# Two graph layers on one core: adjacency combined among the third graph's queries, outputs added a step later, scales reordered, tail in halves

## The chip, the cores and the metric

The kernel runs on one core of a Trainium2 chip. The metric is the time on the device in microseconds (us), from the first to the last instruction of the core. A core has five engines with an instruction queue each: TensorE (PE: matmuls, transposes), VectorE (DVE), ScalarE (ACT), GpSimd (POOL) and SyncE (SP, which here only issues transfers). Each runs its own instructions in the order in which the program gives them, and waits on semaphores for the others. Transfers run on 16 DMA engines.

## What is computed

Sixteen graphs `x` of 1024 nodes with 256 channels go through two layers; everything is float32. Cut to what matters:

```python
# layer 0, for each graph
h = relu(layernorm(x))
c = mean of h over channels
Wg = adj * A_s(c[m] - c[n])              # a weight for each pair of nodes
q = relu((h^T @ Wg) * para)              # queries, four heads of 64
k, v = h @ kv_w
x = x + softmax(q k^T * scale) v         # attention among 1024 nodes

# layer 1
h = relu(layernorm(x))
agg = A_hat @ h                          # A_hat: adj + I, scaled by degrees, the same for all graphs
y = agg @ W1.T + b1
y = relu(batchnorm(y))                   # statistics over all nodes of all graphs
out = batchnorm(y @ W2.T + b2)           # again over all graphs
x = x + out
```

The batch norms need all sixteen graphs before they can scale anything. So the kernel has a first stage (`layers`: layer 0, and layer 1 up to the matmul with W1, graph by graph), a second stage (`second`: the products with W2), and a tail that scales, transposes and adds.

## The kernel before

**First stage.** TensorE alternates between the attention of graph b and pieces of background work for other graphs. A graph has four units (two pairs of heads, two halves of the queries), a unit four steps. A step makes scores, finishes what is due, multiplies the step before's exponentials with the values, and then takes background pieces until their share of TensorE's time is used up:

```python
for s in range(len(steps) + 2):
    ...
        made = scores(*unit.at, g)            # TensorE, then exp on ScalarE
        due = total * (s % per_graph + 1) / per_graph
    finished, ended = ended, None
    if finished is not None:
        finished.finish()                     # transposes of the unit's output, added to x
    if top:
        done += advance(bg)
    ...
        for pr in made:
            unit.add(pr)                      # VectorE sums the exponentials
    if before is not None:
        (last, g_last), prs = before
        last.values(g_last, prs)              # TensorE; the last one copies o to os
        if g_last == NG - 1:
            last.divide()                     # sums, four reciprocals, os * inv
            ended = last
    while done < due and not top:
        cost = advance(bg)                    # a piece of background work
        ...
    if finished is not None:
        finished.watch()                      # two reductions over the reciprocals
```

Background work is made of generators; `weave(main, (start, side), ...)` takes one piece of each side after every piece of the main one, and what is left of the sides at the end. While graph 1's attention runs, the third graph's queries, keys and values are made, and the normalized adjacency is made once for all graphs:

```python
def background(b):
    ...
    gather = aggregate(b - 1)
    if b + 1 < B:
        whole = graph() if b == 1 else nothing
        yield from weave(queries(b + 1), (0, weighers[b + 1]), (0, islice(whole, 16)))
        if b > 1:
            yield next(gather)
        yield from weave(keys_values(b + 1), (0, normed(b - 1)), (0, whole))
        if b == 1:
            yield next(gather)
```

`queries` has 16 pieces, `keys_values` 8. The first piece of `gather` issues the first three loads of adjacency. `graph()` makes the adjacency in eight units. Products with it use a scheme of seven multiplications for a product of 2 by 2 blocks (in place of eight), so differences of its blocks are stored with it, in `aht_d` in HBM:

```python
def graph():
    for t in range(HT):                       # 4
        for part in range(2):
            a = p4.tile([P, 2, NH, HB], F32, tag="adj", ...)      # one of four buffers
            for n in range(2):
                nc.sync.dma_start(out=a[:, n], in_=adj_t...)
            yield 0.0
            for n in range(2):
                ...                           # + identity, * degrees: VectorE
            sub(two[:, 0], b12, a[:, 0, 0])   # sub: GpSimd
            sub(two[:, 1], b22, two[:, 0])
            yield 0.0
            sub(b12, b22, b12)
            sub(one, b21, two[:, 1])
            nc.gpsimd.dma_start(out=dst[:, :4], in_=a...)
            nc.gpsimd.dma_start(out=dst[:, 4:6], in_=two)
            nc.gpsimd.dma_start(out=dst[:, 6], in_=one)
            yield 0.0
```

The four buffers `adj` also hold the blocks of `adj` that `weigh` multiplies with the pair weights (tile `w`, line 382, VectorE), which `queries` uses, and later the pieces `aht` that `aggregate` loads. The banks for `queries` (`pg`) are two; VectorE frees one by writing `q` from it.

**Second stage.** It begins with combinations of W2's blocks on GpSimd, then the scales of the first batch norm, whose square root is on GpSimd as well (`rsqrt`, lines 82 and 83):

```python
nc.gpsimd.tensor_add(s1, a21, a22)
nc.gpsimd.tensor_sub(s2, s1, a11)
nc.gpsimd.tensor_sub(s3, a11, a21)
nc.gpsimd.tensor_sub(s4, a12, s2)
aff = []
for half in range(2):
    r = slice(half * JH, (half + 1) * JH)
    aff.append(affine(mv1[:, r], g1[:, r], be1[:, r], f"1{half}"))
```

Then ScalarE scales and clips `yin`, and TensorE makes seven products for each graph (line 997).

**Tail.** The second batch norm's scales, then graph by graph: scale the whole of both channel halves (1024 nodes each), transpose, add to the graph `xo` of the first layer (loaded from `x1_d`), and store. Up to eight graphs `xo` are held; the ninth is loaded once a store has freed a buffer:

```python
for k in range(CC):
    nc.vector.bn_aggr(mv2[:, k, :], ...)
s2, sh2 = affine(mv2, g2, be2, "2")
for b in range(B):
    while len(xos) < min(b + 8, B):
        load_x1()
    xo = xos[b]
    for k in range(CC):
        nc.scalar.activation(y2[b][k], y2[b][k], AF.Identity, bias=..., scale=...)
    for g in range(NT // 2):
        ...                                   # four transposes
        nc.vector.tensor_add(dst, pt, dst)
    nc.gpsimd.dma_start(out=out[b]..., in_=xo)
```

Of the kernel before, what the change touches and what calls it, by code (L numbers as in the profile page):

```python
# [10 lines left out]
F32 = mybir.dt.float32  # L11
# [6 lines left out]
P = 128  # L18
# [5 lines left out]
def gnn_two_layers_kernel(  # L24
# [60 lines left out]
    def layers(shifted):  # L85
# [135 lines left out]
        def graph():  # L221


            HT, HB = NT // 2, FB // 2
            for t in range(HT):
                for part in range(2):
                    cols = slice(part * HB, (part + 1) * HB)
                    a = p4.tile([P, 2, NH, HB], F32, tag="adj", name=f"au_{t}_{part}")
                    for n in range(2):
                        r = slice((t + n * HT) * P, (t + n * HT + 1) * P)  # L230
                        nc.sync.dma_start(
                            out=a[:, n], in_=adj_t[r].rearrange("p (m c) -> p m c", m=NH)[:, :, cols]
                        )
                    yield 0.0
                    for n in range(2):
                        if part == t * P // HB:
                            blk = a[:, n, n, t * P % HB : t * P % HB + P]
                            nc.vector.tensor_add(blk, blk, ident)
                        nc.vector.tensor_mul(
                            a[:, n], a[:, n], dbc.rearrange("p (m c) -> p m c", m=NH)[:, :, cols]  # L240
                        )
                    two = py.tile([P, 2, HB], F32, tag="y", name=f"two_{t}_{part}")
                    one = py.tile([P, HB], F32, tag="y", name=f"one_{t}_{part}")
                    b12, b21, b22 = a[:, 0, 1], a[:, 1, 0], a[:, 1, 1]
                    sub = nc.gpsimd.tensor_sub
                    sub(two[:, 0], b12, a[:, 0, 0])
                    sub(two[:, 1], b22, two[:, 0])
                    yield 0.0
                    sub(b12, b22, b12)
                    sub(one, b21, two[:, 1])  # L250
                    dst = aht_d[:, t // TH, :, t % TH, cols].rearrange("i p c -> p i c")
                    nc.gpsimd.dma_start(out=dst[:, :4], in_=a.rearrange("p n m c -> p (n m) c"))
# [3 lines that stand above are left out]
# [357 lines left out]
        def background(b):  # L613

            nothing = iter(())
            if b == 0:
                yield from prepare(1, nothing)
                yield from weave(queries(1), (0, weighers[1]), (1, degrees()))
                cbs = columns_of(dinv, "deg")
                if B > 2:  # L620
                    load_x(2)
                    yield from weave(keys_values(1), (1, Norm(2, True).all()))
                else:
                    yield from keys_values(1)
                yield TOP
                broadcast_row(dbc, cbs, "deg")
                yield 1.0
                if B > 2:
                    yield from prepare(2, nothing)
                return  # L630
            before = hidden(b - 1)
            gather = aggregate(b - 1)
            if b + 1 < B:
                whole = graph() if b == 1 else nothing
                yield from weave(queries(b + 1), (0, weighers[b + 1]), (0, islice(whole, 16)))
                if b > 1:
                    yield next(gather)
                yield from weave(keys_values(b + 1), (0, normed(b - 1)), (0, whole))
                if b == 1:
                    yield next(gather)  # L640
            else:
                yield from weave(endings.pop(), (2, normed(b - 1)))
                yield next(gather)
            if b + 2 < B:
                yield from weave(gather, (7, Norm(b + 2, True).all()))
                yield from prepare(b + 2, before)
            elif b + 2 == B:

                yield from gather
                endings.append(before)  # L650
            else:
                yield from gather
                yield from weave(before, (0, normed_last()))
# [156 lines left out]
        def attention():  # L810
# [1 line left out]
            units = [Unit(b, k, f) for b in range(B) for k in range(CC) for f in range(NH)]  # L812
            steps = [(u, g) for u in units for g in range(NG)]
            per_graph = CC * NH * NG
            before = ended = None
            bg, done, total, top = iter(()), 0.0, 0.0, False
            for s in range(len(steps) + 2):
                if s < len(steps):
# [11 lines left out]
                    due = total * (s % per_graph + 1) / per_graph  # L830
                else:
                    due += 5.1
                finished, ended = ended, None
                if finished is not None:
                    finished.finish()
                if top:
                    done += advance(bg)
# [4 lines left out]
                if before is not None:  # L842
                    (last, g_last), prs = before
                    last.values(g_last, prs)
                    if g_last == NG - 1:
                        last.divide()
                        ended = last
                while done < due and not top:
                    cost = advance(bg)
                    if cost is None:  # L850
                        break
                    if cost == TOP:
                        top = True
                        break
                    done += cost
                    if ended is not None and cost > 1.0:
                        ended.behind_piece()
# [41 lines left out]
    def second(kind):  # L899
# [5 lines left out]
        io = st.enter_context(tc.tile_pool(name=f"io_{kind}", bufs=4))  # L905
        ps = st.enter_context(tc.tile_pool(name=f"ps_{kind}", bufs=4, space=PSUM))

        def affine(mv, gamma, beta, name):

            n = mv.shape[1]  # L910
            sm = wp.tile([P, 4, n], F32, name=f"sm_{name}")
            s, sh, rstd, tmp = (sm[:, i, :] for i in range(4))
            rsqrt(rstd, mv[:, :, 1], EPS, tmp)
            nc.vector.tensor_mul(s, rstd, gamma)
            nc.vector.tensor_mul(sh, mv[:, :, 0], s)
            nc.vector.tensor_sub(sh, beta, sh)
            return s, sh

        xos = []

        def load_x1():


            b = len(xos)
            pool, tag = ((xp, "xo"), (io, "yin"), (wp, "both"))[(b % 8 > 2) + (b % 8 > 6)]
            xo = pool.tile([P, NT, C], F32, tag=tag, name=f"xo_{kind}_{b}")
            nc.sync.dma_start(out=xo, in_=x1_d[b])
            xos.append(xo)

        with st:  # L930
            JH = HC // 2


            a11, a12, a21, a22 = (
# [5 lines left out]
            nc.gpsimd.tensor_sub(s2, s1, a11)  # L940
            nc.gpsimd.tensor_sub(s3, a11, a21)
            nc.gpsimd.tensor_sub(s4, a12, s2)
            aff = []
            for half in range(2):
                r = slice(half * JH, (half + 1) * JH)
                aff.append(affine(mv1[:, r], g1[:, r], be1[:, r], f"1{half}"))
            b2_step = wp.tile([P, 1], F32, name="b2_step")
            nc.vector.tensor_sub(b2_step, b2[:, 1:2], b2[:, 0:1])
            ys, t1s, t2s, y2 = {}, {}, {}, []
# [52 lines left out]
            def graph(b, ahead):  # L1002
# [31 lines left out]
                add(c12, product(f"m3_{b}", s4, b22), c12)  # L1034
                stats(1, 1, c22)
                next(ahead, None)
                add(c21, product(f"m4_{b}", a22, t2s[b]), c21)
                stats(0, 1, c12)
                stats(1, 0, c21)
                next(ahead, None)  # L1040

            def ahead_of(b):
# [15 lines left out]
                        load_y(2 * b + 2 + i)  # L1058
                yield

            for i in range(4):
                load_y(i)

# [14 lines left out]
                if kind == "f" and b == B // 2 + 2:  # L1078
                    flag(ps.tile([P, FB], F32, tag="pz", name=f"good_{kind}")[:, 0:1])

            mv2 = wp.tile([P, CC, 2], F32, name="mv2")
            for k in range(CC):
                nc.vector.bn_aggr(mv2[:, k, :], stats2[:, k].rearrange("p a s -> p (a s)"))
            s2, sh2 = affine(mv2, g2, be2, "2")
            for b in range(B):
                while len(xos) < min(b + 8, B):
                    load_x1()
                xo = xos[b]
                for k in range(CC):
                    nc.scalar.activation(  # L1090
                        y2[b][k],
                        y2[b][k],
                        AF.Identity,
                        bias=sh2[:, k : k + 1],
                        scale=s2[:, k : k + 1],
                    )
                for g in range(NT // 2):
                    pt = ps.tile([P, 2, C], F32, tag="pz", name=f"pt_{kind}_{b}_{g}")
                    for j in range(2):
                        t = 2 * g + j  # L1100
                        for k in range(CC):
                            nc.tensor.transpose(
                                pt[:, j, k * P : (k + 1) * P],
                                y2[b][k][:, t * P : (t + 1) * P],
                                ident,
                            )
                    dst = xo[:, 2 * g : 2 * g + 2, :]
                    nc.vector.tensor_add(dst, pt, dst)  # L1108
                nc.gpsimd.dma_start(out=out[b].rearrange("(t p) c -> p t c", p=P), in_=xo)

    fp = ctx.enter_context(tc.tile_pool(name="fp", bufs=1))
    bad = fp.tile([1, 1], mybir.dt.int32, name="bad")
# [61 lines left out]
```

## Time and profile before

| | |
|---|---|
| time, median of three runs | 2741.65 us (2741.38 to 2742.55) |
| span of the profiled execution | 2741.2 us |
| TensorE's mean granted clock | 0.986 |
| HBM read, written | 278.41 MB, 74.45 MB |
| start of the attention, of the second stage's matmuls, end of those | about 65, 2464.2, 2660 us |

A line of the waits reads: the waiting engine, tile and source line, what ended the wait, us in total, how many waits, the longest. A line of the timeline reads: start, duration, engine, source line, operation, output and inputs, shapes, count, and in brackets the idle time of the engine ahead of it and what ended it. A row of the stage table gives the busy time of each engine in a stretch, then TensorE's granted clock, the share of the DMA engines and what they moved in GB/s. A 128x512 line is 128 partitions of 512 elements.

### The profile page before, as it was taken

How to read it: one execution, taken by the hardware profiler on the slowest of the kernel's cores; microseconds unless marked ns; L12 is line 12 of the kernel's file. 1: busy time of each engine (PE TensorE's matmuls, PEld its weight loads, DVE VectorE, ACT ScalarE, POOL GpSimd, SP SyncE). 2: the span in 40 equal slices, each digit the busy share in tenths (PEclk: the TensorE clock that was granted, in tenths of full speed). 3: DMA queues.
4: the chain of work that ended last, by engine and by line, in shares of the span. 5: the costliest groups of instructions: out<-in, count | busy, mean ns of one | idle time of the engine just before them, and what ended most of it. 6: DMA issues, size and time to landing. Idle time of an engine off the chain costs nothing.

```text
span 2741.2 us, 31973 instructions
## 1 busy us (share of the span) xinstructions
PE 2622.6 (96%) x12106; PEld 972.1 (35%) x12106; DVE 1741.1 (64%) x2621; ACT 1293.1 (47%) x1843; POOL 349.2 (13%) x410
## 2 busy tenths in 40 slices
PE   7997999999999999999999999999999999989985
PEld 3332333333333333333333333333333333324444
DVE  5677566666566666666666666666666666646765
ACT  5653354536354454545363545444353634325544
POOL 0016000000010100000000101000000001025652
PEclk9999999999999999999999999999999999999997
DMA  4415424233332414142332324242424313354549
GB/s 154 154 61 186 170 77 156 91 123 100 111 127 84 147 62 161 70 158 89 130 110 99 123 95 136 70 158 65 158 89 142 105 62 116 112 211 184 200 169 369
DMA packets 126051, 355.04 MB, mean 130 GB/s; under 512 B 11456, under 2 KB 32448, under 8 KB 117696
## 3 DMA queue, kind: packets, MB, share of 16 engines
q1 hardware_dynamic: 106816, 278.44, 30.0%
q0 software_dynamic: 19072, 74.46, 7.1%
q8 instruction: 98, 1.61, 0.2%
q14 instruction: 65, 0.53, 0.1%
HBM read 278.41 MB, written 74.45 MB: 129 GB/s over the span
## 4 chain that ended last, share of the span: by engine, by line
PE 88%; DVE 6%; issue 2%; DMA 2%; POOL 1%; ACT 1%; SPq 0%; POOLq 0%; DVEq 0%
PE o L749 17%; PE sc L708 16%; PE pg L149 16%; PE pa L149 13%; PE m_f L997 7%; PE py L149 6%; PE pk L149 4%; PE pv L149 3%; DVE inv L775 3%; PE sums L766 2%; PE ot L802 1%; PE htp L353 1%; DMA xo_f<-x_d 1%; DVE xo_f L1108 1%; PE cbp_c L192 1%
## 5 line engine op out<-in xcount | busy, mean ns | idle before, releaser
L716 ACT ACTIVATE p<-sc 128x1024 f32<-128x1024 f32 x512 | 496.3, 1021 | 728.6 <-PE sc L708 728.5
L738 DVE TENSOR_TENSOR acc<-acc,p 128x1024 f32<-128x1024 f32 x384 | 471.2, 1227 | 161.5 <-ACT p L716 140.4
L708 PE MATMUL sc<-q,k 64*128 64x512 f32 x2048 | 511.0, 617 | 0.5 <-ACT p L716 0.5
L749 PE MATMUL o<-p,v 128*64 128x512 f32 x2048 | 496.0, 605 | 0.0
L149 PE MATMUL pg<-w,h_a 128*64 128x512 f32 x2048 | 453.4, 592 | 1.1 <-DVE q L433 1.1
L149 PE MATMUL pa<-aht,h_b 128*64 128x512 f32 x1536 | 348.2, 595 | 20.2 <-DMA aht<-aht_d 19.5
L708 PEld LDWEIGHTS sc<-q,k 64*128 64x128 f32 x2048 | 176.8, 186 | 322.3 <-issue 271.0
L149 PEld LDWEIGHTS pg<-w,h_a 128*64 128x64 f32 x2048 | 147.9, 137 | 292.6 <-issue 280.8
L775 DVE RECIPROCAL inv<-sums 128x128 f32<-128x128 f32 x256 | 223.9, 921 | 23.1 <-PE sums L766 23.1
L149 PE MATMUL py<-at,w 128*64 128x512 f32 x1024 | 230.8, 592 | 1.0 <-ACT y L565 1.0
L749 PEld LDWEIGHTS o<-p,v 128*64 128x64 f32 x2048 | 124.3, 136 | 286.0 <-issue 286.0
L735 DVE TENSOR_TENSOR acc<-p,p 128x1024 f32<-128x1024 f32 x64 | 78.4, 1225 | 221.4 <-ACT p L716 221.4
L395 ACT ACTIVATE w<-cbc,csum 128x512 f32<-128x512 f32 x256 | 170.1, 714 | 75.8 <-PE pg L149 75.7
L149 PEld LDWEIGHTS pa<-aht,h_b 128*64 128x64 f32 x1536 | 110.9, 137 | 235.4 <-issue 228.9
L382 DVE SCALAR_TENSOR_TENSOR w<-w,adj 128x1024 f32<-128x1024 f32 x128 | 155.8, 1217 | 44.0 <-ACT w L403 44.0
L565 ACT ACTIVATE y<-py,vec 128x512 f32<-128x512 f32 x128 | 87.6, 684 | 183.6 <-PE py L149 156.0
L566 POOL DMA_DIRECT2D y_d<-y x128 | 70.6, 552 | 710.7 <-ACT y L565 707.5
L403 ACT ACTIVATE w<-w 128x1024 f32<-128x1024 f32 x128 | 134.7, 1052 | 1.7
L149 PEld LDWEIGHTS py<-at,w 128*64 128x64 f32 x1024 | 73.9, 137 | 146.8 <-issue 137.8
L149 PE MATMUL pv<-kvw,ht 128*64 128x256 f32 x1024 | 116.2, 379 | 0.4 <-DVE v L470 0.4
L569 DVE BATCH_NORM_STATS2 stats<-y 128x6 f32<-128x512 f32 x128 | 84.8, 679 | 49.6 <-ACT y L565 47.7
L149 PE MATMUL pk<-ht,kvw 128*64 128x512 f32 x512 | 115.5, 593 | 0.0
(133 smaller groups left out, 2366.0 us busy)
## 6 DMA issues: line engine op xcount, KB each, us to landing
aht<-aht_d SPq DMA_DIRECT2D x224, 512.0 KB, 4.3
adj<-in_adj_dram SPq DMA_DIRECT2D x128, 512.0 KB, 4.3
y_d<-y POOLq DMA_DIRECT2D x128, 256.0 KB, 2.8
yin_f<-y_d SPq DMA_DIRECT2D x32, 1024.0 KB, 6.2
x<-in_x_dram SPq DMA_DIRECT2D x32, 512.0 KB, 4.8
para<-in_para_dram SPq DMA_DIRECT2D x64, 256.0 KB, 4.1
x_d<-x POOLq DMA_DIRECT2D x16, 1024.0 KB, 4.2
xo_f<-x_d SPq DMA_DIRECT2D x16, 1024.0 KB, 8.4
```

The source lines that it names most:

```text
L149: nc.tensor.matmul(dst[r], left[:, r], right, start=start, stop=stop)
L382: nc.vector.scalar_tensor_tensor(w, w, 1.0, a, op0=ALU.add, op1=ALU.mult)
L395: nc.scalar.activation(w[:, t, :], cbc[:, q * FB : (q + 1) * FB], AF.Abs, bias=csum[:, th * TH + t : th * TH + t + 1], scale=-1.0,)
L403: nc.scalar.activation(made[i], made[i], AF.Tanh, scale=-0.5 / C)
L565: nc.scalar.activation(y, made, AF.Identity, bias=b1[:, j : j + 1])
L569: nc.vector.bn_stats(stats1[:, j, i, :], y)
L708: nc.tensor.matmul(sc[:, e, :], ks[b][k][r, m * P : (m + 1) * P], qs[b][k][r, f * FB : (f + 1) * FB], start=True, stop=True,)
L716: nc.scalar.activation(pr, sc, AF.Exp)
L738: nc.vector.tensor_add(self.acc, self.acc, pr)
L749: nc.tensor.matmul(self.o[r, :], vs[b][k][:, m, r], pr[:, e, :], start=(m == 0), stop=(m == NT - 1),)
L775: nc.vector.reciprocal(self.inv[:, c], self.pt[:, c])
L997: nc.tensor.matmul(made, left[:, j, :], right[:, j, :], start=(j == 0), stop=(j == JH - 1))
```

## The change

There are four parts, each meant to take away an idle time of TensorE or of DMA.

1. The adjacency's units take two pieces each instead of three, so that all eight fit beside the 16 pieces of the third graph's queries; the first loads of adjacency are then issued before keys and values in every graph.
2. A unit's output is transposed and added two steps after its sums instead of one, except in the last graph.
3. The scales of the first batch norm come before the combinations of W2's blocks. Those of the second are made in two parts: the first channel half's statistics and root are asked for before the last addition of the last graph.
4. The tail works in halves of graphs: loads and stores are of half a graph, and the very first scalings too. Three more graphs `xo` are held, in the buffers of the first three graphs' `y2` once those are done.

```diff
@@ graph()
                     sub(two[:, 1], b22, two[:, 0])
-                    yield 0.0
                     sub(b12, b22, b12)
@@ background(b)
-                yield from weave(queries(b + 1), (0, weighers[b + 1]), (0, islice(whole, 16)))
-                if b > 1:
-                    yield next(gather)
-                yield from weave(keys_values(b + 1), (0, normed(b - 1)), (0, whole))
-                if b == 1:
-                    yield next(gather)
+                yield from weave(queries(b + 1), (0, weighers[b + 1]), (0, whole))
+                yield next(gather)
+                yield from weave(keys_values(b + 1), (0, normed(b - 1)))
@@ attention()
-                finished, ended = ended, None
-                if finished is not None:
+                finished = ended = None
+                if pending and pending[0][1] <= s:
+                    finished, _ = pending.pop(0)
                     finished.finish()
 ...
                         ended = last
+                        pending.append((last, s + (2 if last.at[0] < B - 1 else 1)))
@@ second(): affine in two parts, begin (rsqrt) and finish (three operations on VectorE); load_x1 in halves
+            if not 8 <= b < 11:
+                pool, tag = ((xp, "xo"), (io, "yin"), (wp, "both"))[(b % 11 > 2) + (b % 11 > 6)]
 ...
+                    yp.tile([P, HT, C], F32, tag=f"y2_{b - 8}_{i}", name=f"{name}_{i}")
 ...
+            for i in range(2):
+                nc.sync.dma_start(out=halves[i], in_=x1_d[b][:, i * HT : (i + 1) * HT, :])
@@ second(): the affine of the first batch norm moved ahead of the four combinations
@@ graph(b, ahead) of the second stage
-                add(c21, product(f"m4_{b}", a22, t2s[b]), c21)
+                m4 = product(f"m4_{b}", a22, t2s[b])
                 stats(0, 1, c12)
+                if b == B - 1:
+                    scales(0)
+                add(c21, m4, c21)
                 stats(1, 0, c21)
@@ tail
+            scales(1)
+            for _, finish, _ in affs:
+                finish()
 ...
+                for part in range(2 if b == 0 else 1):
+                    n = slice(part * FB, N if b > 0 else (part + 1) * FB)
+                    for k in range(CC):
+                        s2, sh2 = affs[k][2]
+                        y = y2[b][k][:, n]
+                        nc.scalar.activation(y, y, AF.Identity, bias=sh2, scale=s2)
+                for half in range(2):
+                    xo = xos[b][half]
 ...                                           # transposes and additions of four node blocks
+                    nc.gpsimd.dma_start(
+                        out=out[b].rearrange("(h t p) c -> h p t c", h=2, p=P)[half], in_=xo
+                    )
+                if len(xos) < B:
+                    load_x1()
```

More of the change, by code (lines that the diff above doesn't have):

```diff
@@ L814, in attention @@
             per_graph = CC * NH * NG
-            before = ended = None
+            before = None
+            pending = []
             bg, done, total, top = iter(()), 0.0, 0.0, False
@@ L906, in second, with affine_parts @@
         ps = st.enter_context(tc.tile_pool(name=f"ps_{kind}", bufs=4, space=PSUM))
-        def affine(mv, gamma, beta, name):
+        def affine_parts(mv, gamma, beta, name):
             n = mv.shape[1]
@@ L912, in affine, with finish @@
             s, sh, rstd, tmp = (sm[:, i, :] for i in range(4))
[L913 to L917, printed above, removed]
+            def finish():
+                nc.vector.tensor_mul(s, rstd, gamma)
+                nc.vector.tensor_mul(sh, mv[:, :, 0], s)
+                nc.vector.tensor_sub(sh, beta, sh)
+            return lambda: rsqrt(rstd, mv[:, :, 1], EPS, tmp), finish, (s, sh)
+        def affine(*args):
+            begin, finish, both = affine_parts(*args)
+            begin()
+            finish()
+            return both
         xos = []
@@ L924, in load_x1 @@
             b = len(xos)
[L925 to L928, printed above, removed]
+            name = f"xo_{kind}_{b}"
+            HT = NT // 2
+            if not 8 <= b < 11:
+                pool, tag = ((xp, "xo"), (io, "yin"), (wp, "both"))[(b % 11 > 2) + (b % 11 > 6)]
+                xo = pool.tile([P, NT, C], F32, tag=tag, name=name)
+                halves = [xo[:, :HT, :], xo[:, HT:, :]]
+            else:
+                halves = [
+                    yp.tile([P, HT, C], F32, tag=f"y2_{b - 8}_{i}", name=f"{name}_{i}")
+                    for i in range(2)
+                ]
+            for i in range(2):
+                nc.sync.dma_start(out=halves[i], in_=x1_d[b][:, i * HT : (i + 1) * HT, :])
+            xos.append(halves)
         with st:
             JH = HC // 2
+            aff = []
+            for half in range(2):
+                r = slice(half * JH, (half + 1) * JH)
+                aff.append(affine(mv1[:, r], g1[:, r], be1[:, r], f"1{half}"))
             a11, a12, a21, a22 = (
@@ L942, in second @@
             nc.gpsimd.tensor_sub(s4, a12, s2)
[L943 to L946, printed above, removed]
             b2_step = wp.tile([P, 1], F32, name="b2_step")
@@ L1059, in ahead_of, with scales @@
                 yield
+            mv2 = wp.tile([P, CC, 2], F32, name="mv2")
+            affs = []
+            def scales(k):
+                nc.vector.bn_aggr(mv2[:, k, :], stats2[:, k].rearrange("p a s -> p (a s)"))
+                c = slice(k, k + 1)
+                affs.append(affine_parts(mv2[:, c, :], g2[:, c], be2[:, c], f"2{k}"))
+                affs[k][0]()
             for i in range(4):
@@ L1079, in second @@
                     flag(ps.tile([P, FB], F32, tag="pz", name=f"good_{kind}")[:, 0:1])
[L1081 to L1084, printed above, removed]
-            for b in range(B):
-                while len(xos) < min(b + 8, B):
-                    load_x1()
[L1088 to L1109, printed above, removed]
@@ new lines, in second @@
+            scales(1)
+            for _, finish, _ in affs:
+                finish()
+            while len(xos) < min(8, B):
+                load_x1()
+            for b in range(B):
+                for part in range(2 if b == 0 else 1):
[4 more added lines that the diff above has]
+                        nc.scalar.activation(y, y, AF.Identity, bias=sh2, scale=s2)
+                for half in range(2):
+                    xo = xos[b][half]
+                    for g in range(NT // 4):
+                        pt = ps.tile([P, 2, C], F32, tag="pz", name=f"pt_{kind}_{b}_{half}_{g}")
+                        for j in range(2):
+                            t = half * NT // 2 + 2 * g + j
+                            for k in range(CC):
+                                nc.tensor.transpose(
+                                    pt[:, j, k * P : (k + 1) * P],
+                                    y2[b][k][:, t * P : (t + 1) * P],
+                                    ident,
+                                )
+                        dst = xo[:, 2 * g : 2 * g + 2, :]
+                        nc.vector.tensor_add(dst, pt, dst)
+                    nc.gpsimd.dma_start(
+                        out=out[b].rearrange("(h t p) c -> h p t c", h=2, p=P)[half], in_=xo
+                    )
+                if len(xos) < B:
+                    load_x1()
```

## The prediction

> **What bounds the kernel now.** I read the page's busy shares first, then the list of what TensorE waited for, then the timelines around the three longest of those waits and the stage table of the last 80 us. The first line of the page settles what to look for: TensorE is busy for 2622.6 us of a span of 2741.2.
>
> ```profile
> PE 2622.6 (96%) x12106; PEld 972.1 (35%) x12106; DVE 1741.1 (64%) x2621; ACT 1293.1 (47%) x1843; POOL 349.2 (13%) x410
> ```
>
> So 118.6 us without a matmul are all that reordering can win; no part of the diff removes a matmul. The list of TensorE's waits says where they are (waiter, what it waited for, us in total, times, longest):
>
> ```profile
> PE ot L802 <- DVE os L778: 29.6, 20, 1.8
> PE pa L149 <- DMA aht<-aht_d: 19.5, 3, 18.8
> PE cbp_c L192 <- DVE cb_c L181: 14.0, 4, 11.8
> PE pt_f L1102 <- DVE xo_f L1108: 10.9, 4, 6.3
> PE m_f L997 <- POOL sm L83: 8.3, 1, 8.3
> PE pt_f L1102 <- ACT y_f L1090: 7.4, 2, 6.7
> PE htp L353 <- DVE ht L356: 3.5, 1, 3.5
> ```
>
> Each of the four parts of the diff aims at one of these: the output transposes at the first line, adjacency at the second, the scales' order at the fifth, the tail at the fourth and sixth. The third (start of the program) and the last stay.
>
> **The skill.** "TensorE: Matmul & The Clock Gate", What's actually happening: TensorE drops to half clock after an idle window of about 3.4 us and comes back after a busy one. The trace agrees: after the 18.8 us gap the granted clock is 0.50 until 282 us. "SBUF — State Buffer", Who interferes with whom: a VectorE instruction with two SBUF inputs contends with GpSimd's reads. The trace fits: the products `au` on VectorE take 627 to 1129 ns for one shape, GpSimd's `one` 722 to 1725. "DMA: Bandwidth & Descriptors", Measured: 425 GB/s for a large transfer; here 430 between 2660 and 2664 us. "Perfetto Trace Analysis", DMA Optimizations: splitting transfers may let some start sooner where DMA is idle; the tail below is such a place.
>
> **Part 1, outputs a step later.** A unit's output `os` is scaled by VectorE after its four reciprocals (921 ns each). TensorE meets the transposes one step after the sums. In a middle graph this is the only idle time:
>
> ```profile
> 329.92 0.67 DVE L778 TENSOR_TENSOR os<-os,inv 128x512 f32<-128x512 f32 x1
> 330.74 0.63 PE L802 MATMUL ot<-ident,os 128*128 128x128 f32 x4 [1.75 <-DVE os L778]
> ```
>
> The same 1.75 us comes back every 150.06 us, at 480.80, 630.86 and so on to 2131.45: 13 times, 22.75 us. In 330 to 480 us TensorE is busy 148.31 of 150, so nothing else is idle there. With 1.72 and 0.26 in the first graph and 0.16 and 0.46 near the end of the fifteenth, 25.35 us lie ahead of the last graph. A step is 7 to 9 us of TensorE work; `os` is late by 1.75. One step more hides it all. The last graph keeps its old distance, and its three waits (1.35 + 1.44 + 1.44 = 4.23 us) stay. The addition of the output and the two reductions that watch the reciprocals (692 + 676 + 676 ns) only move; VectorE is busy 95.4 of 150 us there. In the last graph the norm of the one before starts a step later, perhaps 0.5 us. **Gain 25.3, less 0.5.**
>
> **Part 2, adjacency.** The wait of 18.8 us:
>
> ```profile
> 264.97 0.58 POOL L254 DMA_DIRECT2D aht_d<-one  x1
> 265.55 0.55 POOL L581 DMA_DIRECT2D x_d<-x  x1
> 270.90 0.94 SPq L155 DMA_DIRECT2D x<-in_x_dram  x2
> 271.95 9.83 SPq L501 DMA_DIRECT2D aht<-aht_d  x5
> 277.75 3.68 PE L149 MATMUL pa<-aht,h_b 128*64 128x512 f32 x8 [18.78 <-DMA aht<-aht_d]
> ```
>
> The last of eight units of combinations is written out at 265, the load of `aht` can be issued at 272 only, and TensorE starts at 277.75, at half clock to about 282: 4.4 us that do the work of 2.2. So the wait is worth 18.8 + 2.2 = 21.0 us.
>
> Before, a unit took three pieces (load, half, half): 24 pieces, 16 of them beside the 16 pieces of queries (189 to about 233 us) and 8 beside keys and values. Now it takes two, 16 in all, and the last falls on the last piece of queries. GpSimd needs per unit, by its rows, 0.86 + 0.87 + 0.90 + 1.15 us of subtractions and 0.82 + 0.71 + 0.58 of issues, 5.9 us; eight take 47 us. Starting at 194.7 it can't be done before about 242; I reckon 250 with waits. With 4.2 us to landing and 4.3 to load, `aht` is there by 259. TensorE wants it no earlier than 258.97 (277.75 - 18.78), and later if anything slips. **The wait goes.**
>
> What may come instead: a load of `au` (3.8 us to landing, up to 5.9) is issued one piece, 1.71 us of TensorE work, before VectorE wants it, and a buffer of four is often freed only just before. In the kernel before, the third piece often put a step boundary between: the load at 198.30 is used at 203.01 without waiting. In the new order VectorE, which runs in order, stands for it at about 198.3, 207.8 and 216, by my hand schedule 4 to 5 us each, because the load waits for the weigher's product that frees `adj`, or for the write of an earlier `au` to land. VectorE is busy 9.6, 8.4, 8.0, 5.3 and 9.1 us in the five tens from 190 to 240: 9.6 us of slack, against some 14 of standing. What it owes then is the product `q`, which frees the two banks of queries, so TensorE should stand behind `q` in the second group of queries; I work it out as 4 to 7 us, plus up to 3.4 at half clock. I take 7. **Gain 21.0 - 7 = 14.0.**
>
> **Part 3, order of the scales.** At the start of the second stage GpSimd does four combinations of weights first, and the square roots that everything waits for come after:
>
> ```profile
> 2458.79 0.74 POOL L939 TENSOR_TENSOR combined<-w 128x256 f32<-128x256 f32 x1
> ...
> 2460.96 0.72 POOL L942 TENSOR_TENSOR combined<-w,combined 128x256 f32<-128x256 f32 x1
> 2461.66 0.23 POOL L82 TENSOR_SCALAR sm<-mv 128x2 f32<-128x2 f32 x1
> ...
> 2464.22 3.75 PE L997 MATMUL m_f<-yin_f,w 128*128 128x512 f32 x4 [8.33 <-POOL sm L83]
> ```
>
> The roots can start at 2458.79, where the combinations stood: 2461.66 - 2458.79 = 2.87 us earlier. The statistics of the last pair end at 2459.72, before the second root. The combinations then end near 2463.7; the first, needed by the second product, near 2461.6, in time. The stage to 2660 is solid TensorE, so all 2.9 us count. The gap shrinks to 5.5 us, still over an idle window, so I count nothing for the clock.
>
> **Part 4, the tail.** From the end of the matmuls (2660) to the end are 81 us. The stage table, two us a row (DMA share and GB/s last):
>
> ```profile
> 2666.00:2668.00 2.00, 0.65 (x2) 0.36 (x3) 0.00 (x0) 2.00 (x3) 0.00 (x0) 0.50 0.18 74
> 2668.00:2670.00 2.00, 2.00 (x10) 2.00 (x11) 1.07 (x2) 2.00 (x3) 0.00 (x0) 0.50 0.00 0
> 2670.00:2672.00 2.00, 2.00 (x14) 2.00 (x13) 1.68 (x4) 2.00 (x3) 0.00 (x0) 0.63 0.00 0
> 2672.00:2674.00 2.00, 2.00 (x20) 1.97 (x19) 2.00 (x5) 2.00 (x3) 0.97 (x1) 1.00 0.06 25
> 2674.00:2676.00 2.00, 1.97 (x16) 1.46 (x15) 2.00 (x4) 2.00 (x3) 0.89 (x1) 1.00 1.02 420
> ```
>
> DMA is idle from 2666.4 to 2673.9, then full until 2737: the end is set by bytes, and only an earlier first byte helps. The waits of TensorE in this list (10.9 and 7.4 us) lie beside full DMA or ahead of that byte, and are no gain of their own. VectorE's work up to the last statistics is unchanged (one addition, two statistics, two aggregations), so the second root ends where the one root did. Then the first half of each scaling (0.80 us for 128x512) is awaited instead of two whole ones (1.23 each), the first beside the second root: 1.7 us earlier; and two additions (0.85 apart) instead of four precede the store: 1.7 more. **Gain 3.4**; the three additional buffers let loads of `x1` start sooner, which moves the same bytes. Halves read 4 KB rows instead of 8; that may cost some tenths.
>
> **Sum.** 25.3 - 0.5 + 14.0 + 2.9 + 3.4 = 45.1 us; 2741.65 - 45.1 = 2696.6, called 2696.
>
> **Rivals.** (a) No new wait in part 2: all 21.0 us come, total 52.1, 2689.5; for it speaks that VectorE waited only 0.9 us for `au` before, against it the missing piece between load and use. (b) VectorE becomes the bound among the queries: stalls chain through `q`, the bank and the half clock and give back 15 us of the 21, and `aht` is late again by a few: about 2705 to 2710. GpSimd's 47 us in a window of 50 speak for it. (c) The transposes' 1.75 us turns into another wait of the same step (exponentials or the bank `t`, one buffer, free for four steps): then 2718; the solid 148.31 us of work speak against it. (d) The tail is hidden anyway: only 3 us.
>
> **Range and chances.** Parts 1, 3 and 4 I trust to 2 us together; part 2 ranges from 5 to 21. That gives 2688 to 2706, widened to 2687 to 2708. Faster by over 2% needs 2687 or less, the best case and a little more: 0.1. Slower by 2% would need a chain I can't see: 0.01.
>
> **What would show it.** Right: the list of waits has `ot` at about 4.2 us in some three waits, no long `pa` for `aht`, `m_f` at 5.5; a period of 148.3 us between graphs; DMA starting on the outputs some 10.5 us after the last matmul of the products instead of 13.9. New in it: `pg` behind `q` for 4 to 7 us between 200 and 245, VectorE idle behind `au`. Wrong: a `pa` wait for `aht` of several us, `pg` over 12 us, or `ot` still above 10.

## The result and the profile after

The changed kernel takes 2699.68 us (median of four runs, 2696.85 to 2700.17), the kernel before 2742.1 beside it: a ratio of 0.9842, 95% interval 0.9825 to 0.9859. That is 42.4 us faster, and 3.7 us slower than the 2696 predicted, inside the range.

From the page of the kernel after, the line that answers to the first one shown of before:

```profile
PE 2620.7 (97%) x12106; PEld 968.3 (36%) x12106; DVE 1742.3 (65%) x2624; ACT 1292.3 (48%) x1845; POOL 363.2 (13%) x428
```

The same 12106 matmuls are busy for the same time within 2 us, while the span fell from 2741.2 to 2698.1: what went was idle time, 118.6 us before and 77.4 now. The list of what TensorE waited for, after (waiter, cause, us in total, times, longest):

```profile
PE cbp_c L192 <- DVE cb_c L181: 14.1, 4, 11.7
PE pg L149 <- DVE q L432: 7.5, 3, 4.7
PE pt_f L1134 <- ACT y_f L1126: 5.8, 2, 5.2
PE m_f L1017 <- POOL sm L83: 4.8, 1, 4.8
PE pt_f L1134 <- DVE xo_f L1140: 4.3, 5, 1.4
...
PE pa L149 <- DMA aht<-aht_d: 2.7, 2, 1.5
...
PE ot L798 <- DVE os L774: 1.4, 2, 1.1
```

The wait for `os` fell from 29.6 us to 1.4, the one for `aht` from 19.5 to 2.7 (two short waits, both in the last graph), the one for the roots from 8.3 to 4.8. The first line, at the start of the program, is touched by no part. One line is new in size: the queries' bank `pg` waits for VectorE's product `q`, 7.5 us, of which 1.1 us was there before.

Laying the starts of the graphs' first scores in both timelines beside each other gives where the 43.1 us of the two spans went:

| stretch | before | after | difference |
|---|---|---|---|
| start to the first scores | 62.58 | 61.86 | -0.7 |
| graph 0 | 120.00 | 118.06 | -1.9 |
| graph 1 (adjacency) | 173.09 | 160.39 | -12.7 |
| graphs 2 to 13, each | 150.06 | 148.27 | -1.79, in all -21.5 |
| graph 14 | 132.31 | 131.61 | -0.7 |
| last graph's scores to the second stage's first product | 175.52 | 171.05 | -4.5 |
| products of the second stage | 195.74 | 195.33 | -0.4 |
| last product to the end | 81.23 | 80.64 | -0.6 |

Two stretches ask for an explanation. Graph 1 had 21.0 us to give by the prediction, and with the 1.75 us of part 1 in it part 2 brought only 10.95. The tail's first store came 3.2 us sooner after the last product (9.1 us against 12.35), and the end hardly moved.

**Graph 1.** The timeline after, among the third graph's queries (start, duration, engine, line, ..., idle before it and its cause):

```profile
208.71 0.29 DVE L238 TENSOR_TENSOR au<-au,ident 128x128 f32<-128x128 f32 x1 [3.32 <-DMA au<-in_adj_t_dram]
...
211.61 0.29 DVE L238 TENSOR_TENSOR au<-au,ident 128x128 f32<-128x128 f32 x1 [1.89 <-DMA au<-in_adj_t_dram]
...
212.55 0.69 DVE L432 TENSOR_TENSOR q<-pg,para 128x512 f32<-128x512 f32 x1
...
213.29 3.68 PE L149 MATMUL pg<-w,h_a 128*64 128x512 f32 x8 [4.72 <-DVE q L432]
...
218.63 3.45 PE L149 MATMUL pg<-w,h_a 128*64 128x512 f32 x8 [1.66 <-DVE q L432]
```

VectorE stands 3.32 and 1.89 us for the two loads of one unit; behind them in its queue is `q`, whose products were complete at 208.57 us, and TensorE stands 4.72 us behind that; then once more 1.66 behind the second `q`. Eight matmuls of `pg` last 1.7 to 1.9 us elsewhere; these two groups take 3.68 and 3.45. The stage table says why (TensorE's granted clock is the third figure from the end):

```profile
213.00:217.00 4.00, 3.68 (x8) 0.77 (x8) 3.90 (x5) 1.86 (x3) 4.00 (x4) 0.50 0.41 138
```

It is the half clock that "TensorE: Matmul & The Clock Gate", What's actually happening, describes after an idle window. So 21.0 - 6.4 (waits) - 3.6 (two groups at half clock) = 11.0, against 10.95 measured.

**The tail.** Rows of the stage table after (last two figures: DMA share and GB/s):

```profile
2626.00:2628.00 2.00, 2.00 (x10) 1.60 (x10) 1.68 (x3) 2.00 (x3) 0.85 (x1) 0.50 0.00 0
2628.00:2630.00 2.00, 1.98 (x17) 1.74 (x16) 1.65 (x4) 2.00 (x3) 0.82 (x2) 0.97 1.00 254
...
2640.00:2650.00 10.00, 9.87 (x68) 6.99 (x67) 10.00 (x18) 10.00 (x9) 2.90 (x4) 1.00 1.02 412
...
2670.00:2680.00 10.00, 0.00 (x0) 0.00 (x0) 2.07 (x4) 0.00 (x0) 5.22 (x7) 0.50 1.03 392
2680.00:2690.00 10.00, 0.00 (x0) 0.00 (x0) 0.00 (x0) 0.00 (x0) 2.31 (x4) 0.50 1.01 341
```

and a row of the kernel before in which stores run alone as well:

```profile
2724.00:2734.00 10.00, 0.00 (x0) 0.00 (x0) 1.83 (x4) 0.00 (x0) 0.89 (x1) 0.50 1.02 397
```

DMA starts on the stores 10.5 us after the last product (2617.5) instead of 13.9, as predicted, and is full from there on. But from its start to the end of the program it now takes 70.1 us (2698.1 - 2628.0) instead of 67.3 (2741.2 - 2673.9). The last loads have landed by 2672, and of the stores that then run alone the later ones move 341 GB/s at a full share. By the trace's packets the last 5.4 MB of stores take 17.6 us in the changed kernel and 14.8 in the kernel before: 2.8 us, as much as the whole lengthening.

### The profile page after: what moved, and what is told of

Same layout as the page of the kernel before. It is cut to its first block, busy times and chain, and to the rows that moved or that the text cites. A ratio compares the mean times of both kernels' runs of the same rounds, so it can differ in the third digit from the quotient of the medians.

```text
span 2698.1 us, 32021 instructions
## 1 busy us (share of the span) xinstructions
PE 2620.7 (97%) x12106; PEld 968.3 (36%) x12106; DVE 1742.3 (65%) x2624; ACT 1292.3 (48%) x1845; POOL 363.2 (13%) x428
## 4 chain that ended last, share of the span: by engine, by line
PE 93%; DMA 3%; DVE 2%; issue 2%; ACT 1%; POOL 0%; SPq 0%; POOLq 0%; DVEq 0%; ACTq 0%
PE sc L704 18%; PE o L745 18%; PE pg L149 16%; PE pa L149 13%; PE py L149 7%; PE m_f L1017 7%; PE pk L149 4%; PE pv L149 4%; PE sums L762 2%; DMA out_dram<-xo_f 2%; PE ot L798 1%; PE htp L352 1%; PE cbp_c L192 1%; DMA y_d<-y 0%; DVE acc L734 0%
## 5 line engine op out<-in xcount | busy, mean ns | idle before, releaser
L82 POOL TENSOR_SCALAR lnsm_b<-mv_b 128x4 f32<-128x4 f32 x32 | 7.3, 230 | 805.2 <-DVE mv_b L277 805.1
L802 DVE TENSOR_TENSOR x<-ot,x 128x512 f32<-128x512 f32 x64 | 44.2, 691 | 110.6 <-PE ot L798 109.8
```

## The experiments

Every kernel was timed in turns with the kernel before, whose medians were between 2741.7 and 2742.95 us. An interval of the ratio is 0.0007 to 0.0017 to each side, 2 to 5 us, so differences of one or two us between kernels are not read from times. Traces vary as well: graph 1 takes 160.39 us in the trace of the changed kernel and 159.1 to 159.4 in four kernels below that differ from it in the tail alone; the tail takes 80.95 to 82.0 us in four kernels that have the old one. A stretch is known to about 1 us.

**Part 1 alone.** The kernel before with the pending list of outputs:

```diff
-                finished, ended = ended, None
+                finished = ended = None
+                if pending and pending[0][1] <= s:
+                    finished, _ = pending.pop(0)
...
+                        pending.append((last, s + (2 if last.at[0] < B - 1 else 1)))
```

> Part 1 alone on the kernel before. Theory (the transposes' waits are hidden and nothing takes their place): the period between graphs falls from 150.06 to 148.3 us, the wait of TensorE for os is 4.3 us or less (the last graph's), and the time falls by 25 to 27 us, to about 2716. Rival (another wait of the same step takes over): the period stays above 149 and the gain is under 15 us.

Measured: 2711.46 us, ratio 0.9886 (0.987 to 0.9903), 31.2 us faster. Period between graphs 148.27. Waits of TensorE:

```profile
PE pa L149 <- DMA aht<-aht_d: 20.5, 3, 18.5
...
PE ot L802 <- DVE os L778: 1.4, 2, 1.1
```

In the middle graphs nothing took the wait's place, and more came than the theory allowed. Most of the excess lies at both ends. In the last graph, which keeps its distance of one step, the waits for `os` fell too, from 4.23 us to 1.4, while those for `aht` rose from 0.7 to 2.0 and those of `py` for `y` from 1.0 to 2.1. Its timeline shows two pieces of background work between sums and transposes where the kernel before had one (8 matmuls):

```profile
2319.77 1.03 PE L766 MATMUL sums<-acc,ones 128*64 128x512 f32 x4
2320.63 3.60 PE L149 MATMUL pa<-aht,h_b 128*64 128x512 f32 x16
```

By the code, the last graph's background includes a norm that waits for the previous graph's output and counts 0.1 for each piece it waits; the output a step later shifts that count, and a piece moves into the steps after the sums. That is argued and not tested; the first unit of the last graph has two pieces there as well and still waits 1.10 us. The last graph's scores to the first product of the second stage went from 175.52 to 173.18 us, 2.3 of the excess; graphs 0 and 1 together gave 5.1 us where their waits for `os` had been 3.7. Another 1.0 us lies in the start, the second stage and the tail, which this part doesn't touch.

**Part 2 alone.** The missing `yield` and the order of `background`, in the kernel before.

> Part 2 alone on the kernel before. Theory (21.0 us of wait and cold clock go; 6.4 us of waiting for q and 3.7 us of half clock come in the second group of queries): a gain of 10 to 12 us, about 2731, with pg waiting for q some 6 us and the clock at 0.5 for two or three windows after it. Rival (part 1, which moves an addition and two reductions of VectorE by a step, is what makes VectorE late there): without part 1 the wait for q is under 3 us and the gain 15 to 19 us, about 2724.

Measured: 2733.57 us, 0.9969 (0.9958 to 0.9981), 9.1 us faster, a little under the 10 to 12 expected.

```profile
PE pg L149 <- DVE q L432: 10.1, 3, 7.0
```

Two of these three, 7.03 and 1.96, are new. So VectorE is late there without part 1, even by 2.6 us more: the rival falls. The cost belongs to part 2 itself.

**Part 3 alone.** The first batch norm's `affine` calls ahead of the four combinations.

> Part 3 alone, the order of the first batch norm's scales only. Theory: the roots stand where the four combinations stood, the wait of m_f for the roots falls from 8.3 to 5.5 or less, gain 2.9 to 3.5 us, about 2738.5. Rival (the combinations, now last, are waited for by the second product, or the clock dip eats it): gain under 1.5 us.

Measured: 2739.97 us, 0.999 (0.9984 to 0.9997), 2.7 us faster (0.8 to 4.4 by the interval).

```profile
PE m_f L997 <- POOL sm L83: 5.4, 1, 5.4
```

8.33 became 5.42, 2.9 us, the time of the four combinations. In the changed kernel and those derived from it the same wait is 4.8 to 6.3 us.

**Part 4 alone.** Tail in halves, scales in two parts, three more buffers.

> Part 4 alone, the second batch norm's scales in two parts and the tail in halves with three more buffers. In the whole change the first store came 3.2 us sooner after the last product, and yet the end only 0.6 us sooner. Theory (the tail's own transfers run slower: the last 20 us are stores alone, at 341 to 392 GB/s instead of 397 to 420): gain of 0 to 1.5 us here as well, about 2741. Rival (the lost time in the whole change is chance of that run, one of its four runs was 3 us faster): gain of 3 us or more, 2739 or less.

Measured: 2741.78 us, 0.9996 (0.9987 to 1.0005). The first store is issued at 2669.35 us, 9.1 after the last product, and the tail is 81.05 us long instead of 81.23. So it is no chance of one run: the earlier start is lost again. The four parts alone sum to 31.2 + 9.1 + 2.7 + 0.9 = 43.9 us, the whole to 42.4: within the intervals they add.

**Where the tail's start is lost.** Three kernels undo one trait of the tail each, in the changed kernel; a fourth leaves loads out. Whole-graph stores after the first graph:

```diff
+                    if b == 0 or len(xos[b]) == 2:      # first graph, and those in y2 buffers
                         nc.gpsimd.dma_start(out=out[b]...[half], in_=xo)
+                    elif half == 1:
+                        nc.gpsimd.dma_start(out=out[b]..., in_=xos[b][2])   # 1 MB
```

> The whole change, but graphs are stored whole (1 MB) except the first one and the three in y2 buffers. Theory A (stores of half a graph are the slow ones at the end): the last 15 us of stores run at some 42 ns per KB and DMA engine instead of 46 to 49, the end comes 1.5 to 2.5 us sooner, about 2697.5. Theory B (the three more buffers make loads end early and leave a long stretch of stores alone, which is slow whatever the size): 47 ns per KB again, 2699 to 2701.

Measured: 2697.3 us, 0.9836 (0.982 to 0.9852). Its tail is 80.34 us by the trace against 80.64, and its stores alone run at 342 GB/s between 2680 and 2690. Their size is not what slows them; theory A falls. The rest of the difference in time lies ahead of the tail, where the two programs are the same, and is no effect of the stores.

Whole-graph loads (`nc.sync.dma_start(out=halves[2], in_=x1_d[b])`):

> The whole change, but graphs are loaded whole (8 KB rows) except the three in y2 buffers; stores in halves. Theory A and B: the last stores stay at 46 to 49 ns per KB, time within 1 us of the changed kernel's 2699.7. Theory C (4 KB rows cost in the first stretch of the tail, where both run): 1 to 2 us faster.

Measured: 2699.5 us, 0.9843 (0.9827 to 0.986), tail 81.41 us. Loads alone, in the six us after the last product, do run faster with 8 KB rows, at 39 ns per KB and DMA engine against 44 (39 in the kernel before), but the tail gains nothing by it.

Eight buffers (`if True:` in place of `if not 8 <= b < 11:`, and tags by `b % 8`):

> The whole change, but eight graphs held as before, without the three more in y2 buffers. Theory B: loads go on longer, stores alone fall to some 12 us at 42 ns per KB, and the end comes 1 to 2 us sooner, about 2698. Theory A: the last stores stay at 46 to 49 ns per KB and the time at 2699 or above (a later ninth load may cost something too).

Measured: 2697.95 us, 0.9835 (0.9819 to 0.9852), tail 80.52 us, 0.1 less than with eleven; here too the rest of the time is no effect of the tail. Loads go on longer and the stores at the end run alone for 16.8 us instead of 24.4, at 398 GB/s in 2675 to 2680 and 365 in 2680 to 2690; but with the ninth load waiting for a store to land, the start is slow: by the packets 306 GB/s in the second five us of stores, where the changed kernel moves 406. One is bought with the other.

The fourth leaves the tail's second eight loads out altogether, so that graphs 8 to 15 are added to what the buffers of graphs 0 to 7 still hold; half of the output is another sum than the reference's, and only the transfers are of interest:

```diff
+            if b >= 8:
+                xos.append(xos[b - 8])
+                return
```

> The whole change with the second eight loads of x1 left out of the tail: graphs 8 to 15 are added into the buffers of graphs 0 to 7 (half of the output is another sum than the reference's; its time is the question). After the first few us DMA then carries stores only, with no loads at all. Theory B (stores alone are slow by themselves, once they have run alone for some us): over most of the stretch 46 to 50 ns per KB, 335 to 365 GB/s. Theory A2 (the last 15 us are slow because of what had piled up in the queue, or the end of the program): 41 to 43 ns per KB, 395 to 420 GB/s, until the last 15 us.

Measured once: 2684.28 us. Its stage table, with no load in flight:

```profile
2640.00:2650.00 10.00, 9.87 (x69) 7.00 (x68) 10.00 (x18) 10.00 (x10) 5.98 (x8) 1.00 1.00 320
2650.00:2660.00 10.00, 9.78 (x68) 6.81 (x66) 10.00 (x18) 6.59 (x6) 4.25 (x7) 1.00 1.01 328
```

Stores alone move 320 to 332 GB/s from 2640 to 2675, at a full share, slower still than the 335 to 365 expected, and take 49 to 52 ns for each KB on a DMA engine (summed from the trace's packets) instead of 40 to 41 where loads run beside them in the changed kernel. TensorE and ScalarE stop in this stretch and the rate stays. So theory A2 falls: stores alone can be slow anywhere in the tail, and the kernel with whole stores shows that those can be slow, too.

Theory B is only half right, since a long stretch alone is not enough. In the kernel before, stores run alone for the last 15.9 us and take 42 ns per KB to the end; with eight buffers it is 16.8 us, and 46 to 47 ns from about the fourth us on. The number of waiting stores isn't it either: five whole graphs are issued and not landed at 2724 us of the kernel before (397 GB/s) and at 2680 us of the kernel with whole stores (342 GB/s). What makes the stores slow these runs do not say; whole loads, whole stores and eight buffers together, with the earlier start, were not run.

**The cost of part 2.** If VectorE standing for `au` ahead of `q` is the cost, moving a unit's work one piece later should take it away, with not an instruction less:

```diff
                     yield 0.0                       # after the load
+                    yield 0.0
 ...
                     nc.gpsimd.dma_start(out=dst[:, 6], in_=one)
-                    yield 0.0
```

> The whole change, but a unit's VectorE work comes one piece later, two pieces behind its load and behind the product q of that piece, with the last unit right after the last piece of queries. Same instructions, same buffers. Theory (VectorE stands for loads issued one piece ahead, and q queues behind it): the waits of pg for q fall from 6.4 us to under 2.5, the half clock after them goes, and the time falls to 2690 to 2694 (the changed kernel: 2699.7). Rival (VectorE simply has too much to do among the queries, whatever its order): pg still waits 5 us or more, 2698 to 2702.

Measured: 2695.29 us, 0.9827 (0.981 to 0.9843). The `pg` waits fell to one, of 4.5 us, with one window of half clock; of the waits for `au` two are left, 3.6 and 1.1 us. That was half of what the theory expected: the third unit's load needs the first unit's store landed, and VectorE still met it ahead of a `q`. So the third unit alone was moved a piece further:

```diff
+                    if (t, part) == (1, 0):
+                        yield 0.0
```

> As the run with units one piece later, but the third unit's VectorE work yet one piece later, so that the one load still waited for there (3.6 us, it needs the first unit's store landed) stands behind both products q of the first group instead of ahead of one. Theory (in-order VectorE standing for au ahead of q is all of the new cost): no wait of pg for q over 1 us and no half clock between 205 and 225 us, some 6 us faster than with one piece (2695.3): 2688 to 2690.5. Rival (VectorE's amount of work): pg waits as before, 2694 to 2696.

Measured: 2692.59 us, 0.9819 (0.9802 to 0.9835). The stage table where the changed kernel stood still:

```profile
211.00:213.00 2.00, 2.00 (x10) 0.69 (x8) 1.10 (x1) 0.53 (x1) 1.90 (x2) 1.00 0.92 322
213.00:217.00 4.00, 4.00 (x20) 1.34 (x20) 0.82 (x2) 1.41 (x2) 3.79 (x6) 1.00 0.98 324
```

TensorE is busy throughout at full clock, 20 matmuls in the four us that held 8. VectorE still stands for `au`, 1.96 and 2.13 us at 214 and 217, but behind the last `q` of the group (207.98). Graph 1 takes 153.69 us instead of 160.39 (159.1 to 159.4 in the four kernels that differ from it only in the tail). The time is 2 us short of what the theory expected; new in the trace is that VectorE, now later with its copies of `v`, holds TensorE up in keys and values, once for 0.95 us and then for 2.48:

```profile
PE pa L149 <- DVE v L471: 2.5, 1, 2.5
```

Order, not amount, was the cost. This version is clearly faster than the kernel before. Against the changed kernel the medians differ by 7 us, but the intervals of the ratios overlap; the case rests on graph 1, 5.4 to 6.7 us shorter by the traces.

With the two traits of the tail added (whole stores, eight buffers):

> The third unit later (as in the run before this one) with whole-graph stores after the first graph and eight buffers. If the gains add: 2 us from each of the two of the tail at most, more likely 2.5 together as both shorten or ease the same stretch of stores: 2685.5 to 2688. If they are the same 2 us: 2687 to 2689.

Measured: 2692.4 us, 0.9818 (0.9802 to 0.9834), tail 81.18 us against 80.71. Nothing adds, and the expectation is missed by over 3 us: the two traits had hardly shortened the tail by themselves.

**The exception for the last graph.** On top of the third unit later, `s + 2` for every graph and one more turn of the loop:

> On top of the third unit later (2692.6): the last graph's outputs two steps after their sums as well, which the change excepts. Theory (its transposes still wait 1.45 us in all, but the last unit's output is needed at once by the norm of the last graph, so a step there is not hidden): the waits for os go, and a wait for h_b or y of about a step's work less what hidden pieces remain appears; 2692 to 2697, slower by 0 to 4 us. Rival (a step is hidden there too, as in the other graphs): 2691, faster by 1.5 us.

Measured: 2692.69 us, 0.9822 (0.9805 to 0.9838). In the last graph's waits `os` is gone, and in its place stands

```profile
PE pa L149 <- ACT h_b L301: 2.1, 1, 2.1
```

the norm of the last graph, held up by its output. It is as fast with the exception as without; a step there is exchanged, not hidden.

## Why the prediction held, point by point

- **Part 1, predicted 24.8.** The mechanism held: the period went to 148.27 (predicted 148.3), and in the middle graphs no wait took its place. The size was short: 31.2 alone. The mis-sized terms are the last graph, whose three waits the prediction kept at 4.23 us (they are 1.4) and which gave 2.3 us where 0.5 were to be lost; graphs 0 and 1, 5.1 us for 3.7; and 1.79 us a period for 1.75.
- **Part 2, predicted 21.0 - 7.** The wait went, `aht` is loaded in time, and `pg` waits behind `q` as the hand schedule had it: 6.4 us, predicted 4 to 7. The mis-sized term is the half clock: 3.6 us came on top of a wait at the upper end, and taking 7 for both left 3 us out. (In the four kernels that differ only in the tail these waits are 5.5 to 6.3 us and graph 1 is about 1 us shorter.)
- **Part 3, predicted 2.9.** It held: 2.9 us in the wait, 2.7 in the time.
- **Part 4, predicted 3.4.** This step failed. The first store is earlier by 3.2 us as worked out, but "the end is set by bytes, and only an earlier first byte helps" takes a rate for granted. From the first store on DMA was full and took 70.1 us for the bytes that had taken 67.3, because the last stores ran at 341 GB/s instead of 397: 0.6 us came in the whole change. The three buffers that "move the same bytes" did lengthen the stores' stretch alone, from 15.9 to 24.4 us, but the tail without them is as long, so they are not the cause by themselves, and the cause of the slow rate stays open.
- **The sum** of gains was off by only 2.7 us (42.4 for 45.1; the rest of the 3.7 is rounding and the kernel before, 2742.1 beside it). By the parts run alone it was 6.4 us more from part 1 and 4.9, 2.5 and 0.2 less from parts 2, 4 and 3: that these nearly cancel is luck; the mechanisms of parts 1 to 3 stand without it. Of the rivals, (a) and (c) fall (by its own terms (c) stood for about 2719, not 2718); (b), the chain through VectorE, is what happened, smaller than it was drawn and without a late `aht`; (d) is near the truth for part 4, for another reason than a hidden tail.

## What to carry to other kernels

An engine that runs in order makes everything behind a late load late: before work is packed closer, ask what stands behind the instruction that will wait, and put the instruction that frees a bank ahead of it. A gap of TensorE can cost more than its length: here the two of 4.72 and 1.66 us brought 3.6 us of half clock with them, while the 1.75 us before the kernel before's transposes left the clock at 1.00. Where transfers set the end, count their rate and not the bytes alone: a full share of the DMA engines went with 254 GB/s in one place of this tail and with 412 in another.

## What the runs showed of the hardware that was not expected

Stores to HBM that ran without loads beside them moved 320 to 332 GB/s, with the DMA engines at a full share, for 35 us (the run with the second eight loads left out, 2640 to 2675); with loads in flight the two together moved 412 in the changed kernel (2640 to 2650). But it is no rule of stores alone: in the kernel before they keep 397 (2724 to 2734), and in the changed kernel the first ten us still move 392 (2670 to 2680), the next 341. And where the first stores of the tail meet loads, a full share moves as little as 254 GB/s for two us; what delays the packets there stays open.
